# Second expert bias gathered into the row sums, and rows of a pass loaded by units of 32 from ScalarE's queue

## The chip, the core and the metric

The kernel runs on one core of one Trainium2 chip. The metric is the device time of one execution in microseconds (us), as the median of several runs. A profiled execution was taken beside them; every duration below comes from its trace unless something else is said. The engines are called TensorE (PE in the profile; its weight loads PEld), VectorE (DVE), ScalarE (ACT), GpSimd (POOL) and SyncE (SP). A name with a q behind it (SPq, POOLq) is the engine's sequencer or the DMA queue that it issues to.

## The reference

The model is a graph attention network of two layers over 625 nodes and 20000 edges, followed by one transformer block with a mixture of experts, all in float32. Only the last part matters here:

```python
x = x + out @ Wp + bp
h2 = _ln(x, ln2_g, ln2_b).reshape(-1, d)
gate_logits = h2 @ Wg
w, sel = jax.lax.top_k(gate_logits, K)          # K = 1
w = jax.nn.softmax(w.astype(jnp.float32), axis=-1).astype(x.dtype)
combine = jnp.zeros((n, Wg.shape[1]), x.dtype).at[jnp.arange(n)[:, None], sel].add(w)
hid = jax.nn.relu(jnp.einsum('nd,edf->enf', h2, W1) + b1[:, None, :])
y = jnp.einsum('enf,efd->end', hid, W2) + b2[:, None, :]
moe = jnp.einsum('ne,end->nd', combine, y)
return x + moe.reshape(b, t, d)
```

Here d is 768, the hidden width is 3072 and there are 8 experts. With K = 1 the weight of the chosen expert is 1, so each row of the output is the row's sum (the block's input, the attention's residual and the graph network's result) plus `W2[e]` applied to `relu(W1[e] h2 + b1[e])`, plus the second bias `b2[e]`, where e is the row's own expert.

## The kernel before

The 625 rows are five tiles of 125 (`T` = 5, `R` = 125). The graph network and the attention come first and are untouched by the change. What follows is about the end of the attention stage, the first step of the experts, and the loop over the rest.

**Routing (L960 to L1019, L1305 to L1417).** For each tile t, `gate` computes the logits and `choose` writes the expert's number to `ef` (float32) and a one-hot row to `oh`. `send` works out for each row its slot among its expert's rows and scatters the normed row `h2` to the DRAM buffer `xg` (768 floats per row, 640 slots per expert). `send_sums` adds `xx` (attention's part) to `x` and scatters the sum, with the row's number behind it, to the DRAM buffer `xr` (769 floats per row). Both scatters are indirect DMAs from GpSimd's queue. Slots start at `Q` = 32, so that 32 rows ahead of a block may be read as well.

**First step (L1258 to L1285).** The first tile's most frequent expert is taken as `first_e`. Its first 128 rows, from the first three tiles (`TA` = 3), are read back as `xa` (normed rows) and `ra` (sums). While the last two tiles are still being gated, TensorE runs these 128 rows through the expert. One small table is then worked out on VectorE on a single partition (L1320 to L1417): for each pass of the loop a word with the expert's number, a flag for whether its weights are new, and the same for the next pass, and the row at which the pass begins. The pieces of weights `w1[c]` and `w2[c]` (three each, 3.1 MB a piece, each loaded by two DMAs of 1536 KB) fill most of SBUF, in one copy only: a piece of the next expert can be loaded as soon as TensorE has read the present one for the last time. Pieces 1 and 2 lie in the pool `ewb`, whose memory is that of tiles of the attention stage (`xx`, `h2`, `h2T` and others), so their first loads wait for the last reader of these.

**Loop (L1498 to L1549).** A pass handles one block of rows of one expert, made of units of 32 rows: an optional narrow part of one unit (`rq`, bit 0 of the word) and a wide part of none, two or four units (`rw`, bits 1 and 2). At its start a pass

- loads from `xg` the rows of the next pass, always five units (`rows_in`, L1428), by four DMAs from GpSimd's queue, each for a quarter of the columns, into `xb`, which VectorE later turns into `xT` (`turn_next`, L1434);
- loads from `xr` the sums of its own 128 wide rows into `rw` (L1505) and of its 32 narrow rows into `rq` (L1506), from GpSimd's queue;
- then computes: `into` is the first layer on TensorE (L1187 wide, L1461 narrow), `turn` the transposes with ScalarE's `Relu` behind them (L1198, L1203), `out_of` the second layer (L1213 wide, L1476 narrow).

`load_first` and `load_second` (L1152 to L1163) issue the next expert's weights from SP's queue; they are conditional DMAs, skipped where the next pass has the same expert. `load_second` begins with `load_bias`, which loads `b2[e]` into `b2b`, repeated over 128 partitions (384 KB). `prepare` (L1236) copies the rows' numbers and adds `b2b` to the sums; `add_up` adds the second layer's result; `scatter_out` writes the rows to the output.

**What sets the order.** TensorE's instructions are in an order written by hand from the attention stage on, VectorE's between L1053 and L1099, SP's from L785 to L1497. All other instructions are ordered by the framework's scheduler, which works from its own estimates of durations; each engine then executes strictly in order, and an instruction that waits holds up what stands behind it. `tc.issue_after(ins)` puts what is traced in its block, on the engine of `ins`, behind `ins`.

Of the kernel before, what the change touches and what calls it, by code (L numbers as in the profile page):

```python
# [21 lines left out]
R = 125  # L22
T = N // R
# [42 lines left out]
def gnn_moe_kernel(ctx: ExitStack, tc: tile.TileContext, p, out):  # L66
# [630 lines left out]
    with tc.tile_pool(name="att", bufs=1, reuse_waits="tile") as a1, \  # L697
# [241 lines left out]
        def second_norm(t):  # L939
            mv, sd = stats.pop(t)  # L940
            o = h2[:, t, :]
            nc.vector.scalar_tensor_tensor(o, xx[:, t, :], mv[:, 0:1], l2g, op0=OP.subtract,
                                           op1=OP.mult)
            rs = small.tile([R, 1], F32, name="rstd")
            nc.vector.reciprocal(rs, sd)
            nc.vector.scalar_tensor_tensor(o, o, rs, l2b, op0=OP.mult, op1=OP.add)

        h2Ts = {}

# [13 lines left out]


        ef = ap.tile([R, T], F32, name="ef")
        oh = ap.tile([R, T, E], BF16, name="oh")
        io8 = ap.tile([R, E], F32, name="io8")
        nc.gpsimd.iota(io8, pattern=[[1, E]], base=0, channel_multiplier=0,
# [10 lines left out]
        def choose(t):  # L979
            nc.vector.tensor_copy(ef[:, t:t + 1], best(lg[:, t, :]))  # L980
            nc.vector.tensor_scalar(oh[:, t, :], io8, ef[:, t:t + 1], None, op0=OP.is_equal)

        def choose_first():

# [17 lines left out]
        def send(t):  # L1002

            pk = ps.tile([128, 512], F32, tag="tp", name="pk")
            for s in range(t + 1):
                nc.tensor.matmul(pk[:R, :E], before if s == t else ones, oh[:, s, :],
                                 start=(s == 0), stop=(s == t))
            rank = small.tile([R, E], F32, name="rank")
            slot = small.tile([R, 1], F32, name="slot")
            nc.vector.tensor_tensor_reduce(rank, pk[:R, :E], oh[:, t, :], scale=1.0, scalar=0.0,  # L1010
                                           op0=OP.mult, op1=OP.add, accum_out=slot)
            nc.vector.tensor_scalar_add(slot, slot, float(Q))
            nc.vector.scalar_tensor_tensor(pos[t], ef[:, t:t + 1], float(RE), slot, op0=OP.mult,
                                           op1=OP.add)
            scatter(xg, h2[:, t, :], t)

        def send_sums(t):
            nc.vector.tensor_add(x[:, t, :], x[:, t, :], xx[:, t, :])
            scatter(xr, xid[:, t, :], t)  # L1019
# [67 lines left out]
        second_norm(3)  # L1087
        mix(last, (latest,), "tp")
        for t in range(TA):
            send_sums(t)  # L1090
        nc.gpsimd.dma_start(ra, xr[ds(first_e * RE + Q, B), :])
        project(4, 0, all_)
        gate_turn(3)
        project(4, 1, all_)
        gate(3)
        for part in range(2):
            turn_rows(xaT, xa, ps, part, (nc.vector.tensor_copy, nc.scalar.copy)[part])
        second_norm(4)
        pe_order.close()  # L1099

    early.close()
    W1, W2, b2 = p["L0_ffn_W1"], p["L0_ffn_W2"], p["L0_ffn_b2"]
    w1, w2 = [None] * NFC, [None] * NFC

    def piece(ew, l, c):
# [1 line left out]
                                       name=f"ew{l}_{c}")  # L1107

    def load_half(to, e, c, k, **cond):
        nc.sync.dma_start(to, W1[ds(e, 1), :, c * FC:(c + 1) * FC]  # L1110
                          .rearrange("o (p k) f -> p (o k) f", p=128)[:, k:k + 3], **cond)

    def load_piece(e, l, c, **cond):
        if l:

            of_e = W2[ds(e, 1), c * FC:(c + 1) * FC, :].rearrange(
                "o (k two p) d -> two p (o k) d", two=2, p=128)
            to = w2[c].rearrange("p (k two) d -> two p k d", two=2)
            for i in range(2):
                s = nc.sync.dma_start(to[i], of_e[i], **cond)  # L1120
            return s
        else:
            for k in range(0, KD, 3):
                load_half(w1[c][:, k:k + 3, :], e, c, k, **cond)
# [164 lines left out]
    first_a = nc.values_load(first[0:1, 0:1], engines=[mybir.EngineType.DVE], min_val=0, max_val=E - 1)  # L1289
    bT, _ = biases(first_a)  # L1290
    step_a = first_step(xaT, bT, ra)
    begun = next(step_a)

    with tc.issue_after(begun.ins):
        for t in range(TA, T - 1):
            send(t)
            send_sums(t)
        gate_turn(T - 1)
        gate(T - 1)
    with tc.issue_after(next(step_a).ins):  # L1300
        send(T - 1)
        send_sums(T - 1)


    pc = ps.tile([128, 512], F32, tag="p1", name="cnt")  # L1305
# [112 lines left out]
    rt.close()  # L1418

    ewb = ctx.enter_context(tc.tile_pool(name="ewb", bufs=1, reuse_waits="tile"))  # L1420
    for l, c in ((0, 1), (1, 1), (0, 2), (1, 2)):
        piece(ewb, l, c)
        first_load = load_piece(first_e, l, c)
# [15 lines left out]
    row_0 = nc.values_load(table[0:1, 1, 0:1], engines=[pool], min_val=0, max_val=NR - U * Q)  # L1439
    rows_in(row_0)  # L1440
    first_made, = step_a
    right.close()
    routing.close()
# [4 lines left out]
    nc.vector.memset(rq[Q:, :], 0.0)  # L1448
# [39 lines left out]
    def word(i, *engines):  # L1488
        return nc.values_load(table[0:1, 0, ds(i, 1)], min_val=0, max_val=2047,
                              **(dict(engines=engines) if engines else {}))  # L1490
# [7 lines left out]
    with tc.For_i(0, n_blk, 1, iteration_sync="reg_based") as i:  # L1498
        w = word(i)
        then = (w >> 4) & 7, (w >> 3) & 1  # L1500
        row, row_next = (nc.values_load(table[0:1, 1, ds(k, 1)], engines=[pool], min_val=0,
                                        max_val=NR - U * Q) for k in (i, i + 1))
# [5 lines left out]
        tc.add_manual_dep(s.ins, first_load.ins.name, ORDER)  # L1508
        of = {M: Wide(M, xT[:, :, Q:Q + M], bT) for M in (64, B)}

        with tc.If((w & 2) == 2) as c64:
            with tc.manual_schedule(engines={PE}):
                of[64].begin()
        with c64.Else():
            with tc.If((w & 4) == 4):
                with tc.manual_schedule(engines={PE}):
                    of[B].begin()
        with tc.If((w & 1) == 1) as c32:  # L1518
            narrow(bT, *then)
        with c32.Else():  # L1520
            nc.vector.memset(iq, N)
            load_first(*then)
        turn_next()

        def scatter_narrow(*others):
            s = scatter_out(rq, iq, Q)
            for o in others:
                tc.declare_no_dep(s.ins, o.ins, reason="other rows")
            tc.add_manual_dep(s.ins, first_load.ins.name, ORDER)

        def finish(M):
            prepare(rw, iw, M)
            with tc.manual_schedule(engines={PE}):
                of[M].end()
            load_second(*then)
            add_up(rw, pw, M)
            s = scatter_out(rw, iw, M)
            tc.add_manual_dep(s.ins, first_made.ins.name, ORDER)
# [42 lines left out]
```

## Time and profile before

| | us |
|---|---|
| three runs | 1032.6, 1035.97, 1037.0 |
| median | 1035.97 |
| profiled execution, its own time | 1035.84 |
| its span, first to last instruction | 1034.0 |
| first step on TensorE (into 0 to the last out_of) | 614.6 to 687.1 |
| loop on TensorE | 688.1 to 1018.6 |
| last output scatter issued | 1021.3 |

| engine | busy us | share of the span |
|---|---|---|
| PE | 971.3 | 94% |
| PEld | 595.9 | 58% |
| DVE | 460.1 | 44% |
| ACT | 301.5 | 29% |
| POOL | 76.9 | 7% |

The mean granted clock of TensorE is 0.983 of its full speed. A timeline row gives start, duration, engine, line, operation, output and inputs, shapes and count; in brackets stands the idle time before it on its engine and what ended it. A row of windows gives a stretch, its length, the busy time and number of instructions of PE, PEld, DVE, ACT and POOL, then the granted clock, the mean busy share of the 16 DMA engines and the GB/s that they moved. A row of waits gives who waited for whom, the time in total, how often, and the longest. A row of DMA issues gives how often a transfer was issued, its size, and the median time from issue to landing.

The DMA issues that the change touches:

| transfer | queue | issued | KB each | median us to landing |
|---|---|---|---|---|
| `xid<-xg` (xb, a quarter of the columns) | POOL | 32 | 120.0 | 6.5 |
| `rw<-xr` | POOL | 7 | 384.5 | 7.8 |
| `rq<-xr` | POOL | 7 | 96.1 | 7.6 |
| `ra<-xr` | POOL | 1 | 384.5 | 6.3 |
| `xr<-xid,pos` (scatter of sums) | POOL | 5 | 375 | 9.5 |
| `b2b<-in_L_ffn_b_dram` | SP | 9 | 384.0 | |
| `ew<-in_L_ffn_W_dram` (half a piece) | SP | 108 | 1536.0 | |

(375 KB is 125 rows of 3 KB; the page gives no size for indirect DMAs.)

### The profile page before, as it was taken

To read this page: it belongs to the slowest core of one execution; us is meant where nothing else is said; L and a number is where in the kernel's file an instruction comes from. 1 tells how busy PE (TensorE), PEld (TensorE's weight loads), DVE (VectorE), ACT (ScalarE), POOL (GpSimd) and SP (SyncE) were. 2 spreads that over 40 slices of the span, in tenths; PEclk is the share of its full clock that TensorE was granted. 3 is DMA by queue.
4 is the path that set the end of the run, shared out by engine and by line. 5 is a ranking of instruction groups with operands and counts; after the bars stand their busy time and mean duration, and the time that the engine had idled before them with its cause. 6 is when DMAs were issued, how large, how long until landed. Compare 5 with 4: busy or idle time off the path is not lost. (4 is left out here: it accounts for less than half of the span.)

```text
span 1034.0 us, 14964 instructions
## 1 busy us (share of the span) xinstructions
PE 971.3 (94%) x4655; PEld 595.9 (58%) x4656; DVE 460.1 (44%) x1340; ACT 301.5 (29%) x753; POOL 76.9 (7%) x129
## 2 busy tenths in 40 slices
PE   6888999999999999999999889999999999999992
PEld 4455466577555555677775655545454646644552
DVE  7877697275376660284555464112111213111212
ACT  6667554263140120344442211101110121102020
POOL 1200100000000010000000021010101010110010
PEclk9999999999999999999999889999999999999997
DMA  9300410300150081999400579410689999999991
GB/s 280 148 1 1 165 31 1 138 1 1 48 104 1 20 210 36 364 413 381 181 1 1 203 241 352 151 42 15 236 314 321 388 375 409 367 374 402 409 388 33
DMA packets 86880, 195.07 MB, mean 189 GB/s; under 512 B 32989, under 2 KB 34660, under 8 KB 86825
## 3 DMA queue, kind: packets, MB, share of 16 engines
q1 hardware_dynamic: 80073, 174.78, 47.2%
q0 software_dynamic: 6672, 19.44, 6.1%
q8 instruction: 29, 0.48, 0.2%
q14 instruction: 26, 0.21, 0.1%
q10 hardware_dynamic: 80, 0.16, 0.1%
HBM read 213.34 MB, written 39.55 MB: 245 GB/s over the span
## 5 line engine op out<-in xcount | busy, mean ns | idle before, releaser
L1213 PE MATMUL pw<-ew,hT 128*64 128x384 f32 (+1 forms) x672 | 160.2, 488 | 4.9 <-PEq L1518 2.0
L1213 PEld LDWEIGHTS pw<-ew,hT 128*64 128x64 f32 (+1 forms) x672 | 100.0, 160 | 59.5 <-issue 15.8
L1187 PE MATMUL ph<-ew,xid 128*64 128x512 f32 (+1 forms) x432 | 127.7, 594 | 1.8 <-SPq L1498 1.0
L1203 ACT ACTIVATE hT<-tph,bT 128x64 f32<-128x64 f32 (+1 forms) x168 | 41.0, 361 | 288.5 <-PE tph L1198 194.4
L1187 PEld LDWEIGHTS ph<-ew,xid 128*64 128x64 f32 (+1 forms) x432 | 53.6, 155 | 65.1 <-issue 58.1
L1190 DVE COPY hb<-ph 128x512 f32<-128x512 f32 x30 | 20.6, 691 | 137.0 <-PE ph L1187 137.0
L533 PE MATMUL agg<-xl,zT 125*125 125x256 f32 (+1 forms) x300 | 79.8, 417 | 1.3 <-ACT zT L522 1.1
L533 PEld LDWEIGHTS agg<-xl,zT 125*125 125x125 f32 x300 | 54.5, 188 | 19.6 <-ACT zT L522 2.6
L1250 DVE TENSOR_TENSOR rw<-rw,pw 64x192 f32<-64x192 f32 (+1 forms) x48 | 12.9, 315 | 106.0 <-PE pw L1213 105.7
L360 PE MATMUL pp<-w,yT 128*125 128x512 f32 x120 | 56.0, 606 | 0.0
L235 ACT ACTIVATE step<-iota,past 125x314 f16<-125x314 f16 x120 | 55.9, 548 | 0.0
L633 PE MATMUL ph<-wr,h1T 128*125 128x384 f32 x160 | 52.8, 486 | 0.0
L595 PE MATMUL ph<-w,h1T 128*125 128x384 f32 x160 | 52.4, 486 | 0.0
L252 PE MATMUL cps<-step,oh 125*125 125x314 f16 x181 | 37.1, 307 | 10.5 <-ACT step L235 7.4
L857 DVE CUSTOM_DVE_ANT_0 e<-sc,later 125x625 f32<-125x625 f32 (+4 forms) x60 | 29.8, 542 | 36.2 <-PE sc L841 36.2
L924 PE MATMUL po<-wpj,aT 128*125 128x384 f32 x120 | 42.8, 505 | 0.4 <-DVE xx L928 0.4
L861 ACT ACTIVATE e<-e,of 125x625 f32<-125x625 f32 (+4 forms) x60 | 35.7, 596 | 23.3 <-DVE of L857 23.2
L170 PE MATMUL ph<-wr,yT 128*125 128x512 f32 x96 | 42.1, 593 | 0.1
L595 PEld LDWEIGHTS ph<-w,h1T 128*125 128x125 f32 x160 | 30.0, 188 | 21.2 <-issue 0.5
L245 DVE TENSOR_SCALAR oh<-iota,drel,upper 125x125 f16<-125x125 f16 x160 | 41.1, 316 | 2.2 <-PE cps L252 2.1
L633 PEld LDWEIGHTS ph<-wr,h1T 128*125 128x125 f32 x160 | 29.8, 188 | 20.8
L252 PEld LDWEIGHTS <-oh 125*125 125x125 f16 x181 | 24.9, 140 | 26.6 <-DVE oh L245 13.6
(344 smaller groups left out, 1336.4 us busy)
## 6 DMA issues: line engine op xcount, KB each, us to landing
ew<-in_L_ffn_W_dram SPq DMA_DIRECT2D x108, 1536.0 KB
xr<-zt SPq DMA_DIRECT2D x5, 3076.0 KB
xg<-zt SPq DMA_DIRECT2D x5, 3072.0 KB
w<-in_L_gnn_W_dram SPq DMA_DIRECT2D x4, 1536.0 KB
wr<-in_L_gnn_Wr_dram SPq DMA_DIRECT2D x4, 1536.0 KB
xid<-xg POOLq DMA_DIRECT2D x32, 120.0 KB, 6.5
b2b<-in_L_ffn_b_dram SPq DMA_DIRECT2D x9, 384.0 KB
rw<-xr POOLq DMA_DIRECT2D x7, 384.5 KB, 7.8
```

The source lines that it names most:

```text
L170: nc.tensor.matmul(pp[:R, :], yT[:, c, cols(t)], part(wr1, KD, c, i, 512), start=(c == 0), stop=(c == KD - 1))
L235: nc.scalar.activation(o, iota[:, :SH + 1], AF.Sign, bias=at, scale=-1.0)
L245: m = nc.vector.tensor_scalar(o, iota[:, :n], at, weight, op0=OP.is_equal, op1=OP.mult)
L252: nc.tensor.matmul(where, target(R, d[:, j:j + 1], w[:, j:j + 1]), step(s[:, j:j + 1], j % 4 != 3), start=False, stop=False, skip_group_ch ...
L360: nc.tensor.matmul(pp[:R, :], yT[:, c, cols(t)], part(w1, KD, c, i, 512), start=(c == 0), stop=(c == KD - 1))
L533: nc.tensor.matmul(self.agg[:R, c0:c0 + n], zT[:, s, :], xl[:, s, x0:x0 + n], start=(s == 0), stop=(s == T - 1))
L595: nc.tensor.matmul(ph[:R, :384], h1T[:, c, cols(t)], part(w2, KH, c, i, 384), start=(c == 0), stop=(c == KH - 1))
L633: nc.tensor.matmul(ph[:R, :384], h1T[:, k, cols(t)], part(wr2, KH, k, i, 384), start=(k == 0), stop=(k == KH - 1))
L924: nc.tensor.matmul(po[t, i][:R, :384], aT[:, c, cols(t)], wpj[i][:, c, :], start=(c == 0), stop=(c == KD - 1))
L1187: mm = nc.tensor.matmul(ph[g * M:(g + 1) * M, :C].rearrange("p (j f) -> p j f", f=128), self.xT[:, k, :], w[:, k, g], start=(k == 0), stop ...
L1203: self.made = nc.scalar.activation(hT[c][:, k, r], tp[:, k, r], AF.Relu, bias=self.bT[:, f:f + 1])
L1213: mm = nc.tensor.matmul(pw[i][g * M:(g + 1) * M, :384], hT[c][:, k, g * M:(g + 1) * M], w[:, self.block(c, g, k), i * 384:(i + 1) * 384], ...
```

## The change

It has four parts.

1. **The second bias joins the sums.** `choose` also writes the expert's number as an integer, `ei`. A new `add_sums(t)` adds `xx` to `x` and then gathers, by an indirect DMA from GpSimd's queue, the row `b2[ei]` for each of the tile's 125 rows into `xx`. `send_sums(t)` then adds `xx` to `x` a second time and scatters as before. `b2b`, its nine loads and the bias add in `prepare` are gone.
2. **The order around it.** In the attention stage `add_sums` takes the place of `send_sums` for tiles 0 to 2; their `send_sums` stand behind the last instruction of `second_norm(4)` on VectorE. Tile 3's `send_sums` is traced behind `gate(4)`, that of tile 4 in the middle of the table, behind the reduction to `rank`; the load of `ra` follows it.
3. **Rows by units.** `rows_in` issues five DMAs from ScalarE's queue, one for each unit of 32 rows, instead of four from GpSimd's for all units. The wide sums `rw` come as two halves of 64 rows.
4. **Loads skipped.** Inside the loop each of these loads is conditional on the pass (for `rows_in` the next pass) having the unit. A table entry behind the last pass is now zero, so nothing is loaded for it. `rq` is cleared whole, since a skipped load leaves what was there.

```diff
@@ choose, send_sums @@
+        ei = ap.tile([R, T], I32, name="ei")
...
         def choose(t):
             nc.vector.tensor_copy(ef[:, t:t + 1], best(lg[:, t, :]))
             nc.vector.tensor_scalar(oh[:, t, :], io8, ef[:, t:t + 1], None, op0=OP.is_equal)
+            nc.vector.tensor_copy(ei[:, t:t + 1], ef[:, t:t + 1])
...
+        def add_sums(t):
+            nc.vector.tensor_add(x[:, t, :], x[:, t, :], xx[:, t, :])
+            nc.gpsimd.indirect_dma_start(
+                out=xx[:, t, :], out_offset=None, in_=p["L0_ffn_b2"],
+                in_offset=bass.IndirectOffsetOnAxis(ap=ei[:, t:t + 1], axis=0))
...
         for t in range(TA):
-            send_sums(t)
-        nc.gpsimd.dma_start(ra, xr[ds(first_e * RE + Q, B), :])
+            add_sums(t)
...
-        second_norm(4)
+        normed_last = second_norm(4)
@@ weights and bias @@
-    def load_bias(e, **cond):
-        nc.sync.dma_start(b2b, b2[ds(e, 1), :].to_broadcast([B, D]), **cond)
...
-    b2b = mw.tile([B, D], F32, name="b2b", bufs=1)
-    load_bias(first_e)
...
         with tc.manual_schedule(engines={SP}):
-            load_bias(e, cond=new)
             for c in range(NFC):
                 load_piece(e, 1, c, cond=new)
...
         nc.vector.tensor_copy(idx[:M], rows.bitcast(I32)[:M, D:D + 1])
-        nc.vector.tensor_add(rows[:M, :D], rows[:M, :D], b2b[:M])
@@ first step @@
+    with tc.issue_after(normed_last.ins):
+        for t in range(TA):
+            send_sums(t)
     begun = next(step_a)
     with tc.issue_after(begun.ins):
         for t in range(TA, T - 1):
             send(t)
-            send_sums(t)
+            add_sums(t)
         gate_turn(T - 1)
         gate(T - 1)
+        for t in range(TA, T - 1):
+            send_sums(t)
     with tc.issue_after(next(step_a).ins):
         send(T - 1)
-        send_sums(T - 1)
+        add_sums(T - 1)
@@ table @@
     v.tensor_reduce(rank, above, AX.X, OP.add)
+    send_sums(T - 1)
+    nc.gpsimd.dma_start(ra, xr[ds(first_e * RE + Q, B), :])
...
-    v.tensor_scalar(tabf[:, 2, :NS], u, 4.0, None, op0=OP.add)
+    v.scalar_tensor_tensor(tabf[:, 2, :NS], u, 4.0, real, op0=OP.add, op1=OP.mult)
@@ rows @@
-    def rows_in(row):
-        rows = xg[ds(row, U * Q), :].rearrange("(b r) (q c) -> q r b c", r=Q, q=4)
-        for q in range(4):
-            nc.gpsimd.dma_start(xb[q * Q:(q + 1) * Q], rows[q])
+    def rows_in(row, w=None):
+        rows = xg[ds(row, U * Q), :].rearrange("(b r) (q c) -> b q r c", r=Q, q=4)
+        for b in range(U):
+            cond = {} if w is None else dict(cond=unit(w, b))
+            nc.scalar.dma_start(xb[:, b, :], rows[b], **cond)
+
+    def unit(w, b):
+        return (w if b == 0 else (w + 2) >> 2 if b < 3 else w >> 2) & 1
...
-    rows_in(row_0)
+    rows_in(row_of(0, ACT))
...
-    nc.vector.memset(rq[Q:, :], 0.0)
+    nc.vector.memset(rq, 0.0)
@@ loop @@
-        rows_in(row_next)
-        nc.gpsimd.dma_start(rw, xr[ds(row + Q, B), :])
-        nc.gpsimd.dma_start(rq[:Q], xr[ds(row, Q), :])
+        rows_in(row_of(i + 1, ACT), word(i + 1, ACT))
+        row = row_of(i, pool)
+        for b in (1, 3):
+            s = nc.gpsimd.dma_start(rw[(b - 1) * Q:(b + 1) * Q], xr[ds(row + b * Q, 2 * Q), :],
+                                    cond=unit(w, b))
+            behind(s, loads[b - 1])
+        nc.gpsimd.dma_start(rq[:Q], xr[ds(row, Q), :], cond=unit(w, 0))
```

`row_of(i, engine)` and `word(i, *engines)` read an entry of the table into a register of the engines named; `behind` records that a transfer has to follow one of the first expert's weight loads.

More of the change, by code (lines that the diff above doesn't have):

```diff
@@ L945, in second_norm @@
             nc.vector.reciprocal(rs, sd)
-            nc.vector.scalar_tensor_tensor(o, o, rs, l2b, op0=OP.mult, op1=OP.add)
+            return nc.vector.scalar_tensor_tensor(o, o, rs, l2b, op0=OP.mult, op1=OP.add)
         h2Ts = {}
@@ L1097, in gnn_moe_kernel @@
             turn_rows(xaT, xa, ps, part, (nc.vector.tensor_copy, nc.scalar.copy)[part])
-        second_norm(4)
+        normed_last = second_norm(4)
         pe_order.close()
     early.close()
-    W1, W2, b2 = p["L0_ffn_W1"], p["L0_ffn_W2"], p["L0_ffn_b2"]
+    W1, W2 = p["L0_ffn_W1"], p["L0_ffn_W2"]
     w1, w2 = [None] * NFC, [None] * NFC
@@ L1109, in load_half @@
     def load_half(to, e, c, k, **cond):
-        nc.sync.dma_start(to, W1[ds(e, 1), :, c * FC:(c + 1) * FC]
-                          .rearrange("o (p k) f -> p (o k) f", p=128)[:, k:k + 3], **cond)
+        return nc.sync.dma_start(to, W1[ds(e, 1), :, c * FC:(c + 1) * FC]
+                                 .rearrange("o (p k) f -> p (o k) f", p=128)[:, k:k + 3], **cond)
     def load_piece(e, l, c, **cond):
@@ L1118, in load_piece @@
             to = w2[c].rearrange("p (k two) d -> two p k d", two=2)
[L1119 to L1124, printed above, removed]
-    def load_bias(e, **cond):
-        nc.sync.dma_start(b2b, b2[ds(e, 1), :].to_broadcast([B, D]), **cond)
+            return [nc.sync.dma_start(to[i], of_e[i], **cond) for i in range(2)]
+        return [load_half(w1[c][:, k:k + 3, :], e, c, k, **cond) for k in range(0, KD, 3)]
     ewa = ctx.enter_context(tc.tile_pool(name="ewa", bufs=1, reuse_waits="tile"))
@@ L1420, in gnn_moe_kernel, with behind @@
     ewb = ctx.enter_context(tc.tile_pool(name="ewb", bufs=1, reuse_waits="tile"))
+    loads = []
     for l, c in ((0, 1), (1, 1), (0, 2), (1, 2)):
         piece(ewb, l, c)
-        first_load = load_piece(first_e, l, c)
+        loads += load_piece(first_e, l, c)
+    first_load = loads[-1]
+    def behind(s, first):
+        tc.add_manual_dep(s.ins, first.ins.name, ORDER)
     free = xid_all.rearrange("p t d -> p (t d)")
@@ L1437, in turn_next, with word, row_of @@
                                    xb.rearrange("p b (r j) -> p b j r", r=Q))
-    row_0 = nc.values_load(table[0:1, 1, 0:1], engines=[pool], min_val=0, max_val=NR - U * Q)
-    rows_in(row_0)
+    def word(i, *engines):
+        return nc.values_load(table[0:1, 0, ds(i, 1)], min_val=0, max_val=2047,
+                              **(dict(engines=engines) if engines else {}))
+    def row_of(i, engine):
+        return nc.values_load(table[0:1, 1, ds(i, 1)], engines=[engine], min_val=0,
+                              max_val=NR - U * Q)
+    ACT = mybir.EngineType.Activation
+    rows_in(row_of(0, ACT))
     first_made, = step_a
@@ L1486, in narrow @@
             nc.vector.tensor_add(yq[:Q, i, :], rs[:Q, i, :], rs[Q:, i, :])
-    def word(i, *engines):
-        return nc.values_load(table[0:1, 0, ds(i, 1)], min_val=0, max_val=2047,
-                              **(dict(engines=engines) if engines else {}))
     word_0 = word(0, SP)
@@ L1500, in gnn_moe_kernel @@
         then = (w >> 4) & 7, (w >> 3) & 1
-        row, row_next = (nc.values_load(table[0:1, 1, ds(k, 1)], engines=[pool], min_val=0,
-                                        max_val=NR - U * Q) for k in (i, i + 1))
-        rows_in(row_next)
-        nc.gpsimd.dma_start(rw, xr[ds(row + Q, B), :])
-        nc.gpsimd.dma_start(rq[:Q], xr[ds(row, Q), :])
+        rows_in(row_of(i + 1, ACT), word(i + 1, ACT))
[5 more added lines that the diff above has]
+        nc.gpsimd.dma_start(rq[:Q], xr[ds(row, Q), :], cond=unit(w, 0))
         bT, s = biases((w >> 8) & 7)
-        tc.add_manual_dep(s.ins, first_load.ins.name, ORDER)
+        behind(s, first_load)
         of = {M: Wide(M, xT[:, :, Q:Q + M], bT) for M in (64, B)}
@@ L1528, in scatter_narrow @@
                 tc.declare_no_dep(s.ins, o.ins, reason="other rows")
-            tc.add_manual_dep(s.ins, first_load.ins.name, ORDER)
+            behind(s, first_load)
         def finish(M):
@@ L1537, in finish @@
             s = scatter_out(rw, iw, M)
-            tc.add_manual_dep(s.ins, first_made.ins.name, ORDER)
+            behind(s, first_made)
             scatter_narrow(s)
```

## The prediction

> **What bounds the kernel now.** I read the chain of waits first, then who waited for whom, then TensorE's timeline, then short windows. The chain's parts by line begin:
>
> ```profile
> PE 8%; DMA 8%; SPq 4%; issue 0%; DVE 0%; DVEq 0%
> ```
>
> It covers a fifth of the span, 806 to 1022 us, and consists of weight transfers, SP's issue of them, and matmuls. TensorE's timeline names the seven passes of the loop by their shapes: 64 rows (688.1), 128 (723.1), 64 (789.1), 64+32 (823.2), 64 (875.6), 128+32 (911.3), 32 alone (996.9). I number them 0 to 6. TensorE waits for weights five times:
>
> ```profile
> 854.52 4.27 PE L1476 MATMUL pq<-ew,hq 128*32 128x384 f32 x46 [2.38 <-DMA ew<-in_L_ffn_W_dram]
> 907.26 4.09 PE L1213 MATMUL pw<-ew,hT 128*64 128x384 f32 x24 [0.95 <-DMA ew<-in_L_ffn_W_dram]
> 914.94 7.96 PE L1187 MATMUL ph<-ew,xid 128*128 128x512 f32 x18 [0.82 <-DMA ew<-in_L_ffn_W_dram]
> 959.77 4.28 PE L1476 MATMUL pq<-ew,hq 128*32 128x384 f32 x46 [2.10 <-DMA ew<-in_L_ffn_W_dram]
> 1012.65 5.97 PE L1476 MATMUL pq<-ew,hq 128*32 128x384 f32 x46 [3.29 <-DMA ew<-in_L_ffn_W_dram]
> ```
>
> Together 9.5 us: no relief of the transfers can bring more. Four of the landings (854.4, 907.1, 959.6, 1012.5) lie 52.6 to 52.9 us apart, whichever shape the pass has, so from about 792 on the transfers set the pace. Two-microsecond windows (core totals; DMA share and GB/s at the end) show what a pass's rows cost in that state:
>
> ```profile
> 880.00:882.00 2.00, 2.00 (x12) 1.29 (x10) 0.69 (x1) 0.00 (x0) 0.62 (x1) 1.00 1.03 399
> 884.00:886.00 2.00, 2.00 (x11) 0.93 (x7) 0.00 (x0) 0.00 (x0) 1.14 (x3) 1.00 1.07 382
> 886.00:888.00 2.00, 2.00 (x12) 0.90 (x12) 0.69 (x1) 0.94 (x5) 0.00 (x0) 1.00 1.06 238
> 888.00:890.00 2.00, 2.00 (x12) 0.72 (x10) 0.00 (x0) 0.81 (x4) 0.00 (x0) 1.00 1.04 237
> ```
>
> At 881 to 886 GpSimd issues four xb transfers (491 kB), rw (394 kB) and rq (98 kB). Against 400 GB/s the windows fall short by (18+162+163) x 2 us = 0.69 MB, or 1.7 us; the rows' own 0.98 MB take 2.5. A pass's rows cost 4.2 us: ten units of 98 kB, 0.42 each. A b2b (393 kB at 400 GB/s) costs 0.98.
>
> **The loop.** Old rows in pass i: xb of pass i+1 (5 units), rw (4) and rq (1) of pass i. New: only the units that the pass has; b2b is gone. The other price is that of a new xb unit, p. It leaves from ScalarE's queue as one transfer whose source leads with four quarters of 32 short rows; all xb, rw and rq rows of this trace lead with 32 or more on both sides. Nothing like it is shown, so bounds: 0.42, if it spreads as now; 1.68, if each quarter stays together and the 128 packets use a quarter of the engines, which weights need too. I take 1.5, nearer the upper end, because every row at the low price has the other shape.
>
> Saved or lost before each landing:
> - 854.4: xb of pass 3 (3 units, leaving about 768, while the windows from 768 to 792 show shares of 0.78 to 0.93, so half charged: 1.5p), xb of pass 4 (2p), against two old batches (4.2); rw and rq save 3 units in pass 2 and 2 in pass 3 (2.1); b2b 0.98. Sum 3.5p - 7.28 = -2.0.
> - 907.1: xb of pass 5 (5p) against 2.1; pass 4 saves 3 units (1.26); b2b. 5p - 4.34 = +3.2; so far +1.1.
> - 959.6: one xb unit for pass 6, against 2.1; pass 5 needs all its rw and rq; b2b. p - 3.08 = -1.6; so far -0.4.
> - 1012.5: no pass follows (2.1), rw has no unit (1.68), b2b: -4.8; so far -5.2.
>
> TensorE follows: 2.0 early at the first landing, 1.1 late at the second (the 0.82 behind it stays), 0.4 early at the third; at the fourth the weights land 5.2 early, it comes 0.4 early, and the 3.29 are gone. Gain 0.4 + 3.3 = **3.7 us**. At p = 0.42 the sums are -5.8, -8.0, -10.7, -15.5, all five waits go: 9.5. At 1.68: -1.4, +2.7, +1.3, -3.5, a gain of 2.0.
>
> The Trainium skill ("DMA: Bandwidth & Descriptors", section "Why a DMA increments its semaphore by 16 and not by 1") says that a transfer uses the largest number of DMA engines, up to 16, that divides the slowest dimension of both sides. By it a new unit (4 and 128) would run on four; an estimate by that page is the 1.68, and the sum 1034.6; no row here shows it.
>
> Costed at nothing: the ten bias adds of 0.95 us leave VectorE at points where it next waits for TensorE. SP's waits for them (13.1 us in five) go to the weight issue behind, which waits for TensorE's matmuls anyway. ScalarE now issues five conditional transfers per pass ahead of its activations; SP's conditional issue takes about 0.6 us, so some 5 us with the loads of words, in gaps of 18 us or more (868.3 to 887.1 in pass 4); without that cover, TensorE's next weight load waits. If four times as slow as the present 6.5 us, five units land after 26: for pass 5 at about 895, where VectorE turns them from 893.5, but TensorE needs them at 911.3; for pass 0 about 676, needed 688.
>
> **Before the loop.** Here the change adds waits. VectorE: five index copies of 0.15 us; the one of tile 3 stands ahead of the xaT copy, for which TensorE waited 0.98; I charge 0.3 in all. Three more adds of 0.94 behind 616.6 fit into VectorE's idle 6.4 us before 623.0, their gathers landing about 617.6 (issued where the scatters were, 9.5 us to landing). GpSimd issues five more indirect transfers of 1.2 us between waits. ra moves behind the last scatter: landing 641 + 9.5 + 6.3 = 657, used at 673.2.
>
> The last tile is tight. Its index is ready at 634.5, so its gather leaves about 634.9; its add stands behind the table's rank (638.2), and behind it on VectorE come the rest of the table (7.8 us), the memset of rq and the hb copies, for which TensorE already waits:
>
> ```profile
> 647.57 0.70 DVE L1448 MEMSET rq<- 32x769 f32 x1 [1.58 <-DMA xg<-h,pos]
> 649.05 0.66 PE L1198 MATMUL tph<-ident,hb 128*128 128x128 f32 x4 [1.24 <-DVE hb L1190]
> ```
>
> If the gather is S late, the memset starts at 638.2 + S + 0.94 + 7.8 = 646.9 + S instead of 647.6; TensorE loses S - 0.6. Landing takes between 3.1 us (the first output scatter, empty queues) and 9.5 (xr's median): S from 0 to 6.2, loss -0.6 to 5.6. Which is nearer depends on the weights:
>
> ```profile
> SPq L1110 <- PE pl L959: 16.8, 1, 16.8
> xr<-xid,pos POOLq DMA_INDIRECT x5, 9.5
> ```
>
> The first expert's third W1 piece left only at 633.6 and filled the queues until 646, since by the program's allocation its end overlaps h2T by 64 bytes per partition. Without b2b it lies 3,072 bytes lower and waits for second_norm(4) at 616.6; queued behind the others (410 GB/s until 628), it ends about 636. So the gather finds emptier queues: I take S = 1.1, a loss of **0.5**. The last W2 piece (647.5) now also waits for that add at 640, not later; it is needed at 676.6.
>
> **Sum.** Profiled execution 1035.84 (median 1035.97, no difference): 1035.84 - 3.7 + 0.5 + 0.3 = **1032.9 us**.
>
> **Rivals.**
> A, units spread evenly: p = 0.42. For it: same bytes, tile and packet size. Against: the shape. 1035.84 - 9.5 + 0.8 = 1027.1.
> B, ScalarE blocked (the slower side). If issuing from ScalarE meets the full queues as SP does (4.3 us at 827.5, 8.2 at 919.4), pass 4's five issues of t each delay its activations: 868.3 + 2 + 5t + 1.75 against 892.8 costs 5t - 20.7. Later weight waits absorb up to 9.2 with the first gain, so slower than before from t = 5.8. At 8.2: 1035.84 + 20.3 - 9.2 + 0.8 = 1047.7. Against: ScalarE's own queue carries little.
> C, the last gather is late: S = 6.2, loss 5.6: 1035.84 - 3.7 + 5.6 + 0.3 = 1038.0; at p = 1.68, 1039.7. For it: 9.5 us is this scatter's median. Against: the emptier queues.
>
> **Chances.** Forecast 0.44, A 0.32, B 0.12, C 0.12. What a measurement can tell from no change is about 0.5%, 5.2 us. Faster: A but for 0.02, and 0.09 of the forecast (p near 1): 0.39. Slower: 0.11 of B and 0.05 of C: 0.16. Same: 0.45. The range goes from A with no stall (1025.5) to C with the dear unit (1040); the forecast's own is 1030 to 1035.
>
> **What would show it.** The five waits: A leaves none; p near 1.5 leaves a larger one near 907 and none at the last landing. Windows around 868 to 895 show whether five units depress the rate for longer than now. ScalarE's timeline in pass 4 decides B. A VectorE add waiting for a gather behind 638, with a longer TensorE wait near 649, decides C. No dips at all and yet no gain would mean that TensorE's own work sets the pace, and the forecast would be wrong at its root.

## The result, and the profile after

| | before | after |
|---|---|---|
| median of the runs, us | 1035.4 (1032.6 to 1037.0, 4 runs) | 1092.36 (1091.06 to 1097.43, 4 runs) |
| ratio | | 1.0562, 95% interval 1.0521 to 1.0603 |
| profiled execution, us (span) | 1035.84 (1034.0) | 1091.84 (1090.3) |
| TensorE's mean granted clock | 0.983 | 0.957 |
| first step begins | 614.6 | 617.0 |
| loop begins (pass 0) | 688.1 | 704.7 |
| pass 3 begins | 823.2 | 839.4 |
| pass 6 begins | 996.9 | 1061.8 |

The kernel became 5.6% slower, where 0.3% faster was forecast. By these rows the span grew by 56.3 us: 2.4 ahead of the first step, 14.2 in the first step, -0.4 in passes 0 to 2, 48.7 in passes 3 to 5, and -8.6 from the start of pass 6 to the end. The 2.4 are no cost of the change: in the runs below this step begins between 612.3 and 617.4, whatever the edit.

The head of the chain of waits, which covered a fifth of the span before, covers the end alone:

```profile
PE 2%; DVE 0%; issue 0%; DVEq 0%
```

It breaks off at 1061.6, where TensorE waited for a sequencer. A short chain is a hint that waits end at something that the profile can't follow. TensorE's timeline (start, duration, line, operation; in brackets the idle time before, and what ended it) has the waits:

```profile
630.61 1.03 PE L1195 MATMUL tph<-ident,hb 128*128 128x128 f32 x6 [2.82 <-DVE hb L1187]
655.35 0.66 PE L1195 MATMUL tph<-ident,hb 128*128 128x128 f32 x4 [3.66 <-DVE hb L1187]
668.59 7.64 PE L1184 MATMUL ph<-ew,xaT 128*128 128x512 f32 x12 [5.73 <-DMA ew<-in_L_ffn_W_dram]
...
873.69 10.04 PE L1483 MATMUL phq<-ew,xid 128*32 128x256 f32 x144 [17.80 <-issue]
...
938.88 7.35 PE L1210 MATMUL pw<-ew,hT 128*64 128x384 f32 x32 [14.04 <-ACT hT L1200]
...
990.63 1.11 PE L1195 MATMUL tph<-ident,hb 128*128 128x128 f32 x4 [10.87 <-ACT hT L1200]
...
1061.80 9.86 PE L1483 MATMUL phq<-ew,xid 128*32 128x256 f32 x144 [10.46 <-ACTq L1534]
```

All five waits for weights in the loop are gone, and four waits for ScalarE, 53.2 us together, stand in their place (the 17.80 too: `phq` shares its PSUM slot with `tph`, which ScalarE had not read yet). From the start of pass 3 to that of pass 6 TensorE is idle for 53.5 us instead of 8.1 (6.3 of these were waits for weights), and its matmuls take 168.9 us instead of 165.7: that is the 48.7. ScalarE's timeline shows what it did meanwhile:

```profile
867.50 3.78 ACTq L1442 DMA_DIRECT2D xid<-xg  x5
871.74 1.75 ACT L1200 ACTIVATE hT<-tph,bT 128x64 f32<-128x64 f32 x8 [39.75 <-DMA xid<-xg]
...
927.34 10.56 ACTq L1442 DMA_DIRECT2D xid<-xg  x5
938.36 1.75 ACT L1200 ACTIVATE hT<-tph,bT 128x64 f32<-128x64 f32 x8 [37.42 <-DMA xid<-xg]
```

It stood idle for most of 40 us, then issued the row loads of the next pass, and only then ran the Relu that TensorE needed. From the first to the last of the five loads it took 3.8, 10.6, 3.3 and 2.3 us in passes 3 to 6; behind the wait, these 20 us are part of the 53.2. The wait is put down to row transfers. But the rows of the pass before had been turned by 832.8, so neither their landing nor their buffer can have held the issue until 867.5. Who else waits for row transfers, by the waits (us in total, times, longest):

```profile
ACT hT L1200 <- DMA xid<-xg: 140.6, 4, 39.7
...
SPq L1117 <- DMA xid<-xg: 65.8, 7, 33.6
...
DVE xid L1450 <- DMA xid<-xg: 27.3, 1, 27.3
DVE xid L1026 <- DMA xx<-in_L_ffn_b_dram,ei: 10.2, 2, 7.3
```

The second line shows where to look: SP loads weights alone, reads and writes no row, and still waits seven times for rows. A DMA instruction of the trace names the semaphore on which its landing is counted. Those of SP and ScalarE in the loop take eight of them, 140 to 147, in turn, in the order of the program and across both engines; GpSimd's have others (132 to 136). Before an instruction uses a semaphore again, its engine waits until the transfer that had it last has landed. The story of number 140 around pass 3, from the instructions' waits and the semaphore's updates:

```
805.47           SP issues the second half of W2's third piece       (140)
811.61 - 812.18  16 updates: landed
812.34           ScalarE issues row unit 0 of pass 3                 (140)
824.82 - 825.91  4 updates: landed; SP has waited for it since 813.7
826.04           SP issues the second half of W1's second piece      (140)
832.38 - 834.27  16 updates: landed
832.85           ScalarE, at the start of the next rows_in, waits    (140)
847.10           SP issues the second half of W2's third piece       (140)
865.50 - 867.33  16 updates: landed
867.36           ScalarE's wait ends; row unit 0 is then skipped
```

A pass has 5 row loads and 12 halves of weights, 17 transfers on 8 semaphores, and the count starts anew in each pass: the first row load always follows the last half of W2's third piece, the last weights that the pass gets. ScalarE waited for it 34.5, 25.4, 30.0 and 28.7 us in passes 3 to 6; the other four row loads hardly waited. In pass 6 all five loads are skipped, and the wait in front of them cost TensorE 10.46 us all the same: the skip leaves out the transfer, not the wait.

The Trainium skill ("DMA: Bandwidth & Descriptors", section "Why a DMA increments its semaphore by 16 and not by 1") says that on a hardware queue only the engines that a transfer uses report its landing, and that two transfers in flight on one semaphore can't be told apart, so each needs its own. The updates agree: 4 for a row unit, 16 for half a piece. This program shares semaphores and waits instead, and the lines above show the price.

Windows (stretch, its length, busy time and count of PE, PEld, DVE, ACT, POOL; granted clock, DMA share, GB/s) show the rest:

```profile
862.00:868.00 6.00, 0.00 (x0) 0.00 (x0) 0.00 (x0) 0.00 (x0) 0.00 (x0) 0.50 0.60 235
868.00:874.00 6.00, 0.31 (x4) 0.23 (x8) 0.00 (x0) 1.75 (x8) 0.00 (x0) 0.50 0.12 33
874.00:884.00 10.00, 10.00 (x152) 5.78 (x148) 1.02 (x3) 3.61 (x16) 0.00 (x0) 0.80 0.63 236
```

From 862 until the Relu at 871.7 nothing computes, and from 868 the weights' queue is empty as well, since TensorE frees no buffer. The granted clock is 0.50 in the pause and 0.80 in the ten microseconds behind it, and the 144 matmuls at 873.69 took 10.04 us instead of the 7.98 of such a group in the profile before:

```profile
996.91 7.98 PE L1461 MATMUL phq<-ew,xid 128*32 128x256 f32 x144 [0.84 <-DVE rw L1250]
```

In the first step two things went wrong. SP's and VectorE's timelines:

```profile
613.34 1.32 SPq L1117 DMA_DIRECT2D ew<-in_L_ffn_W_dram  x2
615.06 9.74 SPq L1126 DMA_DIRECT2D ew<-in_L_ffn_W_dram  x2
658.74 1.87 SPq L1117 DMA_DIRECT2D ew<-in_L_ffn_W_dram  x2
```

```profile
628.99 0.96 DVE L1026 TENSOR_TENSOR xid<-xid,xx 125x768 f32<-125x768 f32 x1 [7.35 <-DMA xx<-in_L_ffn_b_dram,ei]
...
644.80 0.96 DVE L1026 TENSOR_TENSOR xid<-xid,xx 125x768 f32<-125x768 f32 x1 [2.87 <-DMA xx<-in_L_ffn_b_dram,ei]
```

W1's third piece left at 658.7, 25 us later than before: its semaphore was that of the first row load (`rows_in` of row 0), which ScalarE can issue only when the table is there. It landed 5.73 us too late for TensorE. And VectorE's adds waited for gathers, with the `hb` copies behind them.

### The profile page after: what moved, and what is told of

The parts are those of the page before. It is cut to its first block, busy times and chain, and to the rows that moved or that the text cites. A ratio compares the mean times of both kernels' runs of the same rounds, so it can differ in the third digit from the quotient of the medians.

```text
span 1090.3 us, 15131 instructions
## 1 busy us (share of the span) xinstructions
PE 979.5 (90%) x4655; PEld 594.8 (55%) x4656; DVE 456.5 (42%) x1340; ACT 301.5 (28%) x753; POOL 63.3 (6%) x109
## 5 line engine op out<-in xcount | busy, mean ns | idle before, releaser
L1210 PE MATMUL pw<-ew,hT 128*64 128x384 f32 (+1 forms) x672 | 164.8, 499 | 17.0 <-ACT hT L1200 14.0
L1210 PEld LDWEIGHTS pw<-ew,hT 128*64 128x64 f32 (+1 forms) x672 | 103.3, 163 | 72.4 <-issue 29.4
L1483 PE MATMUL phq<-ew,xid 128*32 128x256 f32 x432 | 27.9, 423 | 28.3 <-issue 17.8
L1246 DVE TENSOR_TENSOR rw<-rw,pw 64x192 f32<-64x192 f32 (+1 forms) x48 | 12.9, 315 | 89.4 <-PE pw L1210 89.2
L252 PE MATMUL cps<-step,oh 125*125 125x314 f16 x181 | 37.3, 309 | 10.6 <-ACT step L235 5.4
```

The source lines that it names most:

```text
L1210: mm = nc.tensor.matmul(pw[i][g * M:(g + 1) * M, :384], hT[c][:, k, g * M:(g + 1) * M], w[:, self.block(c, g, k), i * 384:(i + 1) * 384], ...
L1483: nc.tensor.matmul(v[g * Q:(g + 1) * Q], xT[:, k, :Q], w[:, k, :, g], start=(k == 0), stop=(k == KD - 1))
```

## Experiments

The numbers are the order in which they were set; all ratios are to the kernel before on the same chip. S, N and B name the theories: S, shared semaphores; N, narrow row units that land late; B, the cost of issuing on ScalarE.

### The loop: queue or semaphore (1, 2, 3, 9)

**1. Rows from GpSimd.** The changed kernel with one other queue:

```diff
-            nc.scalar.dma_start(xb[:, b, :], rows[b], **cond)
+            nc.gpsimd.dma_start(xb[:, b, :], rows[b], **cond)
...
-        rows_in(row_of(i + 1, ACT), word(i + 1, ACT))
+        rows_in(row_of(i + 1, pool), word(i + 1, pool))
```

> Changed kernel with the rows' transfers (by units, skipped where a pass lacks them) issued by GpSimd instead of ScalarE, before the loop and in it. Theory S (a row transfer on ScalarE has to wait for the weight transfer that used the same completion semaphore before it, and SP's weights for the rows in turn; GpSimd's transfers have other semaphores): the waits of TensorE of 17.8, 14.0, 10.9 and 10.5 us go, and the 5.73 us wait for weights at 668.6 too; what stays is VectorE's waits for the gathers. 1028 to 1043 us. Theory N (units lead with 4 quarters, so each runs on few DMA engines and lands late, whichever queue it leaves from): the waits move from ScalarE to VectorE's turn of the rows; 1070 to 1095. Theory B (cost of issuing on ScalarE, 2.3 to 10.6 us a pass): 5 issues a pass saved, some 25 us in all: 1060 to 1072.

Measured: 1031.07 us, ratio 0.9964 (0.9949 to 0.9978). No Relu waits for a row transfer any more. TensorE's waits:

```profile
658.36 1.12 PE L1195 MATMUL tph<-ident,hb 128*128 128x128 f32 x4 [9.65 <-DVE hb L1187]
...
915.59 4.09 PE L1210 MATMUL pw<-ew,hT 128*64 128x384 f32 x24 [0.69 <-DMA ew<-in_L_ffn_W_dram]
```

Three of the five weight waits of before are gone; this one and 0.81 us at 923.3 stay. SP issues W1's third piece at once:

```profile
617.62 12.22 SPq L1117 DMA_DIRECT2D ew<-in_L_ffn_W_dram  x2
```

The time lies far below the ranges of N and B, so neither is the main cause. The issues left ScalarE too, so this run alone does not separate S from B, but B was put at some 25 us, and 61 came back. Ahead of the loop something is left: it begins at 699.5, and the wait of 9.65 us before it was 1.24 in the kernel before.

**2. One transfer fewer.** Rows still from ScalarE; the third W2 piece comes in one transfer, so a pass has 16, and the row loads follow other weights on their semaphores.

```diff
+            if c == 2 and cond:
+                return [nc.sync.dma_start(w2[c], W2[ds(e, 1), c * FC:(c + 1) * FC, :].rearrange(
+                    "o (k p) d -> p (o k) d", p=128), **cond)]
```

> Changed kernel; inside the loop the third W2 piece is loaded in one transfer instead of two, same bytes. A pass then has 16 transfers of SP and ScalarE instead of 17, so with 8 completion semaphores in turn the five row transfers of ScalarE share theirs with W1's second piece (last half), W1's third piece and W2's first piece, no longer with the last half of W2's third. Theory S: ScalarE's wait ends some four halves of a piece (4 times 3.9 us) earlier, TensorE's waits of 17.8, 14.0, 10.9, 10.5 us shrink to 5 or less each: 1040 to 1062 us. Theories N and B (late landing by narrow transfers; cost of issuing): nothing about rows or queue is changed: 1085 to 1098.

Measured: 1051.96 us, ratio 1.0181 (1.0149 to 1.0213). Neither a row load nor its queue was touched, and 40 us came back. ScalarE in pass 3, and TensorE's remaining waits:

```profile
832.20 15.24 ACTq L1445 DMA_DIRECT2D xid<-xg  x4
847.90 1.75 ACT L1203 ACTIVATE hT<-tph,bT 128x64 f32<-128x64 f32 x8 [21.07 <-DMA xid<-xg]
```

```profile
865.01 5.95 PE L1501 MATMUL pq<-ew,hq 128*32 128x384 f32 x48 [2.49 <-DMA ew<-in_L_ffn_W_dram]
...
922.75 7.32 PE L1213 MATMUL pw<-ew,hT 128*64 128x384 f32 x32 [5.56 <-DMA ew<-in_L_ffn_W_dram]
...
960.88 1.12 PE L1198 MATMUL tph<-ident,hb 128*128 128x128 f32 x4 [9.14 <-ACT hT L1203]
```

The Relu comes 13.7 us into the pass (834.2) instead of 32.4. In pass 3 ScalarE now waits 2.4 to 5.5 us in front of each unit but the first, as the halves of W1's second and third and W2's first piece land one after the other; in pass 5 it waits 19.3 us in front of the first unit. S holds, though two of TensorE's waits are above the 5 us expected. Of the 21 us that remain against experiment 1, 17.2 are in these three waits.

**3. The kernel before, rows from ScalarE.** Quarters as before, none skipped:

```diff
-            nc.gpsimd.dma_start(xb[q * Q:(q + 1) * Q], rows[q])
+            nc.scalar.dma_start(xb[q * Q:(q + 1) * Q], rows[q])
```

> Kernel before with one thing changed: its four row transfers of a pass (quarters, 32 partitions each, none skipped) leave from ScalarE instead of GpSimd. With b2b a pass has 4 + 13 = 17 transfers on the shared semaphores, so the first quarter follows the last half of W2's third piece on its semaphore, as in the changed kernel. Theory S: ScalarE waits 25 to 40 us in passes 3 to 6 as there: 1065 to 1090 us. Theory N (narrow units are the cause; quarters spread as before): 1030 to 1042. Theory B: four issues a pass instead of five, 1045 to 1070.

Measured: 1072.39 us, ratio 1.0382 (1.0344 to 1.0419). The queue alone makes the old kernel 3.8% slower, with the same waits of TensorE:

```profile
854.09 10.62 PE L1462 MATMUL phq<-ew,xid 128*32 128x256 f32 x144 [15.49 <-issue]
912.31 8.00 PE L1213 MATMUL pw<-ew,hT 128*64 128x384 f32 x32 [6.50 <-ACT hT L1203]
965.55 1.11 PE L1198 MATMUL tph<-ident,hb 128*128 128x128 f32 x4 [11.70 <-ACT hT L1203]
1036.14 10.05 PE L1462 MATMUL phq<-ew,xid 128*32 128x256 f32 x144 [9.97 <-ACTq L1516]
```

Here b2b's transfer makes 4 + 13 = 17, so the first quarter again follows the last weights: ScalarE waits 35.1, 27.5, 36.1 and 29.7 us in passes 3 to 6.

**9. Quarters from ScalarE in the changed kernel.** Without b2b, 4 + 12 = 16 transfers. `rows_in` is that of experiment 3; the rest is the changed kernel.

> Changed kernel; rows still from ScalarE, before the loop and in it, but as the old four quarters (32 partitions each), none skipped. Without b2b a pass then has 4 + 12 = 16 transfers on the shared semaphores, the quarters behind W1's third piece and W2's first, as four of the five units in the second experiment; and SP's loads of these pieces wait for quarters, which spread over all engines. Theory S with SP's waits for late units as the rest of the second experiment's loss (20 us in the loop against the first): some 10 of these 20 us come back, 1036 to 1047 us. If it makes no difference how fast the rows land: 1049 to 1055. If ScalarE's issuing by itself is what costs: 1049 or more.

Measured: 1041.98 us, ratio 1.0063 (1.0042 to 1.0084), in the range of S: 10 us of experiment 2's loss came back, and no wait for weights is left in the loop. One for ScalarE is:

```profile
947.91 1.12 PE L1195 MATMUL tph<-ident,hb 128*128 128x128 f32 x4 [9.28 <-ACT hT L1200]
```

Quarters land sooner. The packets of the five units (491 kB) of pass 5 in each form, with the queues full of weights, from the start of the first to the end of the last; beside them the time from the first issue to the last:

```
                                    packets   issues
quarters, GpSimd   (before)          4.6 us   2.1 us
units,    GpSimd   (experiment 1)   10.0 us   5.4 us
quarters, ScalarE  (experiment 3)    9.6 us   1.7 us
units,    ScalarE  (after)          21.1 us   7.4 us
units,    ScalarE  (experiment 2)   30.9 us  19.6 us
```

The last column shows that the longest spans are in part those of the issuing. For one transfer at a time, experiments 2 and 9 compare best, both with several us between the issues from ScalarE: from issue to landing a unit (98 kB) took 10.8 to 16.3 us, a quarter (123 kB) 6.2 to 6.7.

So N is real, but its cost in experiment 2 is not a wait for rows: SP waits under 2 us for them in the loop. It lies in the weights. A unit's landing is reported by 4 updates, and while units are under way 4 of the 16 updates of the weights are late: of the first half of W2's second piece 12 came at 898.35 to 899.74 and 4 at 907.57 to 907.78. In experiment 9 all 16 came at 895.76 to 898.07. From 860 on SP waits 42.9 us for landings of weights in experiment 2, and 12.9 in experiment 9. Experiment 9 also loads W2's third piece in two transfers again and skips nothing, so the 10 us are not shown to be the shape's alone. VectorE's 27.3 us in the changed kernel, before a turn in pass 4, cost TensorE nothing: the turned rows were there at 955.1, and pass 5 began at 958.0 without a wait.

### The first step (7, 4, 6, 10)

**7. The bias part alone**, with rows as before.

> Kernel before with the bias part alone: b2 gathered and added in the first step in the changed kernel's order, no b2b; rows as before (quarters from GpSimd, none skipped). If the gathers cost what the first experiment shows before the loop (some 10 us) and b2b's transfers are worth 0.98 us each in the loop (4 us in all): 1036 to 1042 us. If b2b brings most of the loop's gain: 1028 to 1035.

Measured: 1035.74 us, ratio 1.0007 (0.9998 to 1.0017); the expected range began 0.3 above. No change at all is a sum: the loop begins 11.7 us later than before, but it takes 6.9 us less, and the time from the last matmul to the end 4.3 us less. The last tile's gather leaves at about the same place as in experiment 1 and TensorE's wait is the same:

```profile
658.45 1.12 PE L1195 MATMUL tph<-ident,hb 128*128 128x128 f32 x4 [9.66 <-DVE hb L1187]
```

**4. Adds behind** (on experiment 1). The add of tile 3 stands behind the copy of `hb` of the second block, that of the last tile behind the table:

```diff
+    with tc.issue_after(copied.ins):
         for t in range(TA, T - 1):
             send_sums(t)
...
-    send_sums(T - 1)
...
+    tabled = v.tensor_copy(table, tabf[:, 2:, :])
+    with tc.issue_after(tabled.ins):
+        send_sums(T - 1)
```

> As the first of these (rows from GpSimd), and VectorE's two adds that wait for late gathers are put behind what TensorE waits for: the add of tile 3 behind the copy of hb of the first step's second block (its wait of 7.35 us held this copy, TensorE lost 2.8), the last tile's add and ra's load behind the table. Theory S with the gathers as the second cost: 3 to 7 us faster than the first of these, loop begins 3 to 7 us earlier: 1023 to 1038 us. If ra's later load holds up the first step instead: no faster than the first.

Measured: 1027.01 us, ratio 0.9927 (0.9901 to 0.9953): 4 us below experiment 1. TensorE still waits 5.72 us for `hb`, since on VectorE the memset of `rq` now holds it:

```profile
643.39 0.96 DVE L1026 TENSOR_TENSOR xid<-xid,xx 125x768 f32<-125x768 f32 x1 [1.28 <-DMA xx<-in_L_ffn_b_dram,ei]
648.38 0.70 DVE L1471 MEMSET rq<- 64x769 f32 x1 [4.03 <-DMA xg<-h,pos]
```

**6. The memset behind too** (on experiment 4):

```diff
-    nc.vector.memset(rq, 0.0)
+    with tc.issue_after(last_copied[0].ins):
+        nc.vector.memset(rq, 0.0)
```

> The fourth experiment (rows from GpSimd, both adds behind), and the memset of rq, which there waits 4.03 us for a scatter with the first step's hb copies behind it, is put behind the last hb copy of the first step. If these 4 us are on the path: TensorE's wait near 650 falls from 5.7 to about 1.2 us, 1021 to 1025 us. If the next thing is late instead (the third W1 piece, ra): as the fourth, 1026 to 1028.

Measured: 1020.26 us (1017.49 to 1023.43), ratio 0.9854 (0.9833 to 0.9874), just below the expected range. The wait is nearly that of the kernel before (1.24) again:

```profile
649.68 0.66 PE L1195 MATMUL tph<-ident,hb 128*128 128x128 f32 x4 [1.41 <-DVE hb L1187]
```

This version has all that the change was to do, with GpSimd's queue for the rows and three instructions of VectorE in other places, and beats both kernels.

**10. The bias part alone with these three in place** (experiment 7, mended as in 4 and 6).

> The seventh experiment (bias part alone, rows as before from GpSimd), with the order of the sixth in the first step: both waiting adds and the memset of rq behind the copies of hb. If the 10.5 us lost there before the loop are all that the bias part costs: loop begins at 688 to 690, 1024 to 1029 us, about 8 below the seventh. If the later loop had hidden waits for weights that now return: 1029 to 1033.

Measured: 1024.68 us, ratio 0.9899 (0.9873 to 0.9925). The first step takes 73.6 us, as before (73.5; 84.1 in experiment 7), so these 10 us were indeed the whole cost of the bias part.

### The rows (5, 8)

**5. The rows alone**: the kernel before with units, halves and skips from GpSimd, b2b kept.

> Kernel before with the rows' part of the change alone, from GpSimd: units of xb, rw in two parts and rq, each skipped where a pass lacks it; the second bias stays as it was (b2b, ten adds). If the rows alone bring most of the loop's gain of the first experiment (three of the five waits for weights gone, 8.4 us), and the gathers all of the time lost before the loop: loop begins as in the kernel before (688), 1025 to 1031 us. If the gain came from b2b's transfers instead: 1031 to 1036.

Measured: 1027.89 us, ratio 0.9936 (0.9920 to 0.9952). The two weight waits in narrow passes come hardly earlier than before (854.5 and 959.8):

```profile
853.93 5.92 PE L1490 MATMUL pq<-ew,hq 128*32 128x384 f32 x46 [2.15 <-DMA ew<-in_L_ffn_W_dram]
...
959.55 4.28 PE L1490 MATMUL pq<-ew,hq 128*32 128x384 f32 x46 [1.11 <-DMA ew<-in_L_ffn_W_dram]
```

Pass 6 begins at 996.8, as before (996.9), so the whole gain is in the last pass, where the wait of 3.29 us is gone and the end is shorter. The time is in the expected range, but one weight wait is gone and not three: the number came out for another reason.

**8. Quarters, none skipped** (on experiment 4): `rows_in` as in the kernel before.

> The fourth experiment, with xb loaded as before the change: four quarters of 32 partitions, none skipped, so 35 units of 98 kB in the loop instead of 17. If a unit at its 4 engines costs about 1.04 us against 0.42 in the old form, both forms cost about the same (17.7 and 14.7 us of transfer): 1024 to 1030 us. If units are as cheap as quarters (0.42): 5 to 8 us slower than the fourth, 1031 to 1036.

Measured: 1030.56 us, ratio 0.9955 (0.9940 to 0.9970). It is 3.5 us slower than experiment 4 by the medians; the upper end of the first case was 1030, the lower of the second 1031. The runs of the two overlap (1025.53 to 1032.59 against 1022.7 to 1028.35), and shape and skipping changed together, so what skipping alone is worth is not shown.

## Why the prediction was wrong, point by point

- **The step that failed** is the one that put ScalarE's five conditional transfers at nothing ("some 5 us ... in gaps of 18 us or more"). The issuing alone would have fitted: 0.13 to 0.18 us for a skipped load, mostly 0.5 to 1.1 for a real one, 10.6 us for all five at the worst. What was missing is the wait in front of them, 25 to 35 us for the last half of the expert's weights; behind it the issuing fits no gap any more. Together they cost TensorE 53.2 us in four waits and about 2 us of slow matmuls behind most of them.
- **Rival B** had the right place and side and another mechanism. "ScalarE's own queue carries little" is true (0.8% of the engines' time in the profile after) and beside the point: it shares semaphores with SP, which carries 172 MB. By its own formula an issue of 3.5 us, the longest seen, would have cost nothing.
- **A sign lay in the profile before.** There SP waits ten times, 19.7 us in the loop, for landings of weights, though the buffers it overwrites are freed by TensorE. I left that unread. It is the same turn of semaphores, on one engine alone: in that trace half a piece lands on number 144 at 852.8 to 854.4, SP's wait for 144 ends at 854.4, and its next transfer, on 144 again, leaves at 854.5.
- **The third W1 piece** was to leave at 616.6 without b2b. With rows from GpSimd it left at 617.6, so the reasoning held; in the changed kernel the shared semaphore held it until 658.7.
- **The last gather** (S = 1.1, loss 0.5; bounds 0 to 6.2) was mis-sized. In experiment 1 the queues are full of that very W1 piece, which landed at 652.1 and not at 636, the gather takes 12 us, VectorE waits 8.87 and TensorE loses 8.4 more than before. That is rival C, beyond its upper end. I had taken the emptier queues; the piece still filled them.
- **Tile 3's add** was not priced at all. Its gather left at 616.7 and VectorE waited 7.35 us with the `hb` copies behind: 2.82 us of TensorE.
- **The price of a unit**, p = 1.5, was near what can be read, but no run gives it for ScalarE's queue free of semaphore waits. With b2b kept, the sums for the first and third landing are 3.5p - 6.30 and 9.5p - 11.76. Experiment 5, whose units leave from GpSimd, moved them by -0.6 and -0.2 us, which gives 1.6 and 1.2 (1.9 and 1.3 if the loop's start, 0.8 us earlier there, is taken off). What was behind the bound of 1.68, a unit on a quarter of the engines, which weights need too, is what the late 4 of 16 updates in experiment 2 show. Five units of pass 5 took 25.7 us from the first issue to the last landing in the changed kernel, where 26 was estimated; but a late landing was no longer free (SP waited for one from 813.7 to 825.9).
- **The loop's gain** of 3.7 us: in experiment 1 the weight waits fall by 8.0 us, but the loop begins 11.3 us later there, so TensorE also asks for weights later. In experiment 6 it begins at 688.8, as before, and they fall by 5.3. There the signs named for p near 1.5 are seen, no wait at the last landing and a larger one near 907, though the first wait stays at 2.0 us where 0.4 were to be left:

```profile
907.88 4.09 PE L1210 MATMUL pw<-ew,hT 128*64 128x384 f32 x24 [1.37 <-DMA ew<-in_L_ffn_W_dram]
```

- **The end**: from the last output scatter's issue to the end of the span took 12.6 us before, 7.2 to 8.3 in all kernels without b2b and 9.4 to 9.9 in those that keep it. This was not foreseen, and its cause stays open. It is no small part: of the 12.1 us by which experiment 6's trace is shorter than that of before, 8.0 lie in the loop and 4.7 behind the last matmul, less 0.6 ahead of the loop. So "no relief of the transfers can bring more" than 9.5 us was too low a bound for the change.

The rows alone give 0.6%, the bias part mended 1.0%, both 1.5%: within the intervals, the two parts add up.

## What to carry to other kernels

Before a transfer moves to another engine's queue, look whose landing is counted on its semaphore before it, and put no in-order engine that feeds TensorE behind a landing that comes last; a conditional load waits even when it is skipped. When an engine waits for a tile that it never touches, as SP here for rows, suspect a shared semaphore and not the tile. What waits for a gather or scatter belongs behind the copies that TensorE needs, and a change that measures as nothing (experiment 7) can be a gain and a loss of ten microseconds each.

## What the runs showed of the hardware that was not expected

- The same 491 kB of rows took 4.6 us as quarters from GpSimd and 21.1 to 30.9 as units from ScalarE, first packet to last, issuing included. In these spans both the shape (4 landing updates for a unit on ScalarE's queue; 128 packets of 768 bytes) and the queue (GpSimd cuts a unit into 20 packets of 4608 and 4 of 1536 bytes) made about a factor of two. That packet size is the reason is argued, not shown.
- While transfers reported by 4 updates were under way, the last 4 of the 16 updates of half a weight piece came about 8 us behind the other 12 (experiment 2); with quarters all 16 came within 2.3 us (experiment 9).
- A wait of TensorE costs more than itself: at a granted clock of 0.50 in the pause, groups behind the waits took 10.04 us instead of 7.98, and 7.35 instead of 5.48.
